# State space layer: dt x B partly from VectorE through PSUM, the product with C wholly on GpSimd, and a new table of half groups

**Chip, cores, metric.** One core of one Trainium2 chip. The metric is the device time of one execution in microseconds (us), median of several runs on the same chip.

## The reference, cut to what matters

Two layers run one after the other. The first is a selective state space layer on 4 images of 64 x 64 positions (4 x 4096 steps in time, 768 inner channels, 16 states), the second a windowed attention. The change touches only the first:

```python
dt = softplus(einsum('blr,dr->bld', dt, dt_w) + dt_b)
def step(h, inp):                     # over the 4096 positions
    dA  = exp(dt_t[:, :, None] * A[None])
    dBx = (dt_t * x_t)[:, :, None] * B_t[:, None, :]
    h   = dA * h + dBx
    y_t = einsum('bdn,bn->bd', h, C_t)
y = y + xc * D;  y = y * silu(z);  out = einsum('bld,cd->blc', y, out_proj_w)
```

## The kernel before

The code here is cut and condensed. In the profiles the engines are DVE (VectorE), POOL (GpSimd), ACT (ScalarE), PE (TensorE) and SP (SyncE); da is the decay exp(dt A), db the product dt x B, hp and hs the state h, and L96 a helper through which most activations go. A hole is time in which the DVE stands idle before a scan.

A step of the kernel is one of 64 chunks of 256 positions (T). In a step there are 24 groups: 6 blocks of 128 channels (d) by 4 groups (g) of 4 states. A group is two half groups of two states; a slot of the schedule is one half group, so a step has 48 slots. All else (projections, convolution, Silu, softplus, output projection of other steps) is hung on these slots, and each engine works its list in order: in the stretch from 2,000 to 4,000 us of the changed kernel's trace the 159 instructions of ACT in a step come in the same order in 19 of 21 steps (the other two have two of a group norm more), GpSimd's 64 in 20 of 21 (the other has a memset in place of a copy).

```python
ps_a bufs=2; ps_h bufs=1; ps_y bufs=2; ps (work banks) bufs=3      # PSUM, 8 buffers

def driven(I, d, g, h):               # dt x B: GpSimd, all 24 groups, [128, 4*256]
    nc.gpsimd.tensor_tensor(db, h["dtx"].unsqueeze(1).broadcast_to([P, NG, T]), h["bc"][g][0], ALU.mult)

def scan(I, d, g, h, db, y, ahead):
    for half, to in ((0, hp), (1, hs)):           # hp in PSUM, hs in SBUF
        da = ps_a.tile([P, 2, T], F32, tag="da")
        for k in range(2):
            act(da[:, k, :], dt, AF.Exp, scale=nega[:, d, n + k : n + k + 1])      # decay
        for k in range(2):
            nc.vector.tensor_tensor_scan(to[:, k, :], da[:, k, :], db[:, 2 * half + k, :], ...)
            if half == 1 and k == 0:
                nc.vector.tensor_copy(state[:, d, n - 2 : n], hp[:, :, T - 1])
                nc.vector.tensor_tensor(hv, hp, ct[:, 0:2, :], ALU.mult)           # C, first half
        ahead()                                   # the other work of this slot
    def with_c():                                 # C, second half: GpSimd
        nc.gpsimd.tensor_copy(state[:, d, n : n + 2], hs[:, :, T - 1])
        nc.gpsimd.tensor_tensor(hs, hs, ct[:, 2:4, :], ALU.mult)
# TensorE sums hv and hs over the states by transposing products into one PSUM tile y per d
# ... slots: x 0-9, conv 11-20, z 20-27, Silu burst 29, softplus 33 + 3q, out_proj 8-10 ...
```

Of the kernel before, what the change touches and what calls it, by code (L numbers as in the profile page):

```python
# [14 lines left out]
P = 128  # L15
C = 384
# [32 lines left out]
def two_layers(  # L49
# [221 lines left out]
    def layer0(x1s, mvs, gms1):  # L271

        with ExitStack() as es:
            es.enter_context(tc.manual_schedule(engines=in_step))
            ps_a = es.enter_context(tc.tile_pool(name="ps_a", bufs=2, space=PSUM))
            ps_h = es.enter_context(tc.tile_pool(name="ps_h", bufs=1, space=PSUM))
            ps_y = es.enter_context(tc.tile_pool(name="ps_y", bufs=2, space=PSUM))
            ps = es.enter_context(tc.tile_pool(name="ps0", bufs=3, space=PSUM))
# [3 lines left out]
            gms, gbs, st1s = {}, {}, {}  # L282

# [17 lines left out]
            def next_batch(b, at):  # L301
# [15 lines left out]
                for n in range(NJ * NXT):  # L317
                    t, j = divmod(n, NJ)
                    at(24 * n + 17, lambda t=t, j=j: load(t, j))
                    at(24 * n + 29, lambda t=t, j=j: nc.vector.bn_stats(st[:, j, t, :], h["x"]))  # L320
# [8 lines left out]
            def normed(I, h, at):  # L329
# [3 lines left out]
                def load():  # L333
                    h["x"] = w2.tile([P, NJ, T], F32, tag="xi", name=f"xi_{b}_{i}", bufs=3)
                    nc.sync.dma_start(
                        h["x"],
                        x[b, :, i * T : (i + 1) * T].rearrange("(k p) t -> p k t", p=P),
                    )
# [30 lines left out]
                at(20, load)  # L369
                at(30, by_group)  # L370
                at(31, lambda: mean("xn", "mu"))
                at(32, lambda: with_row("mu", ALU.subtract))
                at(34, square)
                at(35, lambda: mean("sq", "var"))
                at(37, root)
                at(38, lambda: with_row("var", ALU.mult))
# [21 lines left out]
            def prepared(I, h, at):  # L398
# [13 lines left out]
                def pair(key, first, tile):  # L412
                    def one(k):
                        if k == 0:
                            h["pb"][key] = bank()
                        tile(h["pb"][key], k)

                    at(first, lambda: one(0))
                    at(first + 1, lambda: one(1))

                at(0, kept)
                for p in range(ND // 2):
                    d = 2 * p
                    pair(("x", p), 3 * p, lambda pb, k, d=d: in_proj(pb, k, d + k, h["xn"]))
                    at(3 * p + 3, lambda p=p, d=d: with_bias(
# [8 lines left out]
                    pair(("c", p), 11 + 3 * p, lambda pb, k, d=d: conv(pb, k, d + k))  # L434
                    at(14 + 3 * p, conv_out)

                    def z_out(p=p, d=d):
                        z = w2.tile([P, 2, T], F32, tag="sz", name=f"sz_{b}_{i}_{d}", bufs=5)
                        with_bias(z, h["pb"][("z", p)], binp[:, ND + d : ND + d + 2])
                        h["sz"].append(z)  # L440

                    pair(
                        ("z", p), 20 + 2 * p,
                        lambda pb, k, d=d: in_proj(pb, k, ND + d + k, h["xn"]),
                    )
                    at(23 + 2 * p, z_out)
# [6 lines left out]
                def x_proj():  # L453
                    h["pd"] = bank()
                    for d in range(ND):
# [5 lines left out]
                def rows():  # L461
# [5 lines left out]
                    h["bc"] = []  # L467
                    for g in range(NS // NG):
                        both = []
                        for tag, r0 in (("B", 0), ("C", NS)):  # L470
                            t = bc.tile([P, NG, T], F32, tag=tag, name=f"{tag}_{b}_{i}_{g}")
                            src = rows[r0 + g * NG : r0 + (g + 1) * NG, :]
                            nc.sync.dma_start(t, src.unsqueeze(0).broadcast_to([P, NG, T]))
                            both.append(t)
                        h["bc"].append(both)

                at(29, burst)
                at(30, x_proj)
                at(32, rows)

                def softplus(q, first):
# [27 lines left out]

                    def added():  # L510
                        pb, dt = t["pb"], t["dt"]
                        nc.vector.scalar_tensor_tensor(
                            pb, pb, -1.0, t["e"], ALU.add, ALU.subtract
                        )
                        nc.vector.tensor_tensor(pb, t["r"], pb, ALU.subtract)
                        nc.vector.tensor_tensor(dt, dt, pb, ALU.add)
                        h["dt"].append(dt)

                    at(first, project)
                    at(first + 2, parts)  # L520
                    at(first + 3, exped)
                    at(first + 4, logged)
                    at(first + 5, added)

                for q in range(ND // 2):
                    softplus(q, 33 + 3 * q)

            def driven(I, d, g, h):

                b, i = divmod(I, NCHUNK)  # L530
                if g == 0:
                    h["dtx"] = w2.tile([P, T], F32, tag="dtx", name=f"dtx_{b}_{i}_{d}")
                    nc.gpsimd.tensor_tensor(
                        h["dtx"], h["dt"][d // 2][:, d % 2, :], h["xc"][d // 2][:, d % 2, :],
                        ALU.mult,
                    )
                db = w2.tile([P, NG, T], F32, tag="db", name=f"db_{b}_{i}_{d}_{g}", bufs=3)
                nc.gpsimd.tensor_tensor(  # L538
                    db, h["dtx"].unsqueeze(1).broadcast_to([P, NG, T]), h["bc"][g][0], ALU.mult
                )  # L540
                return db

            def scan(I, d, g, h, db, y, ahead):



                dt = h["dt"][d // 2][:, d % 2, :]
                ct = h["bc"][g][1]
                hp = ps_h.tile([P, 2, T], F32, tag="hp", name="hp")
                hv = w2.tile([P, 2, T], F32, tag="hv", name="hv")  # L550
                hs = w2.tile([P, 2, T], F32, tag="hs", name="hs", bufs=4)
                for half, to in ((0, hp), (1, hs)):
                    da = ps_a.tile([P, 2, T], F32, tag="da", name="da")
                    n = g * NG + 2 * half
                    for k in range(2):
                        act(da[:, k, :], dt, AF.Exp, scale=nega[:, d, n + k : n + k + 1])
                    for k in range(2):
                        nc.vector.tensor_tensor_scan(  # L558
                            to[:, k, :], da[:, k, :], db[:, 2 * half + k, :],
                            state[:, d, n + k : n + k + 1] if I % NCHUNK else 0.0,  # L560
                            ALU.mult, ALU.add,
                        )
                        if half == 1 and k == 0:
                            nc.vector.tensor_copy(state[:, d, n - 2 : n], hp[:, :, T - 1])
                            nc.vector.tensor_tensor(hv, hp, ct[:, 0:2, :], ALU.mult)  # L565
                    ahead()

                def with_c():
                    nc.gpsimd.tensor_copy(state[:, d, n : n + 2], hs[:, :, T - 1])  # L569
                    nc.gpsimd.tensor_tensor(hs, hs, ct[:, 2:4, :], ALU.mult)  # L570

                def summed(t):

                    for k in range(2):
                        first = g == 0 and t is hv and k == 0
                        last = g == NS // NG - 1 and t is hs and k == 1
                        for half in range(2):
                            nc.tensor.matmul(  # L578
                                y[:, half, :], t[:, k, half * P : (half + 1) * P], ident,
                                is_transpose=True, start=(first and half == 0),  # L580
                                stop=(last and half == 1), skip_group_check=True,
                            )

                return with_c, lambda: summed(hv), lambda: summed(hs)

            def turned(I, d, h, yt):

                ys = w2.tile([P, 2, P], F32, tag="ys", name=f"ys_{I}_{d}")
                nc.scalar.copy(ys, yt)
                y = bank()[:, 0, :]  # L590
                for half in range(2):
                    nc.tensor.matmul(
                        y[:, half * P : (half + 1) * P], ys[:, half, :], ident,
                        is_transpose=True, start=(half == 0), stop=False,
                        skip_group_check=True,
                    )
                nc.tensor.matmul(
                    y, dsd[:, d, :], h["xc"][d // 2][:, d % 2, :], start=False, stop=True,
                    skip_group_check=True,
                )  # L600
# [534 lines left out]
```

## Time and profile before

| | before |
|---|---|
| time | 9,142 us (9,140 to 9,145) |
| scans run | 112 us to 6,800 us of the span |
| one step | 104.8 us: DVE busy 93.8, POOL 93.8, PE 83, ACT 71.1 |
| DVE idle in a step | 11.0 us |

The lines are in the prediction below: of the products of 128x512, GpSimd's took 1,269 ns and hv on the DVE, with one operand in PSUM, 681, a ratio of 1.86. All 458 hv of the stretch from 2,000 to 4,000 us took 669 to 685 ns, with GpSimd busy 90% of it. One view it does not show is what ACT waited for in the same stretch (19.1 steps); columns: us in total, times, longest.

```profile
ACT da L96 <- DVE hs L558: 288.8, 270, 3.0
ACT da L96 <- DVE hp L558: 100.1, 201, 2.0
ACT xc L96 <- PE mm_ps L388: 94.4, 19, 5.4
ACT spe L96 <- PE mm_ps L488: 76.7, 19, 4.8
ACT xb L96 <- PE mm_ps L381: 33.5, 36, 1.7
```

The first two lines are harmless: ACT is early and waits for a decay buffer. The next three are not: once a step ACT stands 5 us for the convolution, 4 us for softplus and under 2 us for the projection, the decay behind them in its list is late, and the DVE waits. Measured slot by slot in the trace (idle of the DVE just before the scans of a slot, mean of 55 steps), the holes of before are 3.0 us at slot 15 (convolution), 3.7 at 30 and 31 (Silu burst), 2.5 at 37 to 39 (softplus) and 0.7 at 4.

### The profile page before, as it was taken

How to read it: one execution, taken by the hardware profiler on the slowest of the kernel's cores; microseconds unless marked ns; L12 is line 12 of the kernel's file. 1: busy time of each engine (PE TensorE's matmuls, PEld its weight loads, DVE VectorE, ACT ScalarE, POOL GpSimd, SP SyncE). 2: the span in 40 equal slices, each digit the busy share in tenths (PEclk: the TensorE clock that was granted, in tenths of full speed). 3: DMA queues.
4: the chain of work that ended last, by engine and by line, in shares of the span. 5: the costliest groups of instructions: out<-in, count | busy, mean ns of one | idle time of the engine just before them, and what ended most of it. 6: DMA issues, size and time to landing. Idle time of an engine off the chain costs nothing. (4 is left out here: it accounts for less than half of the span.)

```text
span 9134.5 us, 141565 instructions
## 1 busy us (share of the span) xinstructions
PE 7574.6 (83%) x45882; PEld 5681.8 (62%) x45882; DVE 7496.7 (82%) x15604; ACT 5711.1 (63%) x13566; POOL 7650.8 (84%) x6679
## 2 busy tenths in 40 slices
PE   6877778877778877778877788777879999999999
PEld 5666666666666666666666666666655555555555
DVE  6898888898889888988988888888876666666666
ACT  4666666666666666666666666666644545455454
POOL 5998888988889898889888989988976767777677
PEclk8888878888888888788888788888879999999999
DMA  3111111111111111111111111111112222232222
GB/s 100 53 49 51 54 61 48 48 49 51 58 59 50 50 45 52 59 55 53 49 48 49 58 45 48 45 45 56 51 65 84 89 82 87 83 92 87 82 86 65
DMA packets 301929, 558.05 MB, mean 61 GB/s; under 512 B 61916, under 2 KB 185580, under 8 KB 301060
## 3 DMA queue, kind: packets, MB, share of 16 engines
q1 hardware_dynamic: 301188, 549.00, 18.7%
q8 instruction: 364, 5.96, 0.3%
q14 instruction: 377, 3.09, 0.1%
HBM read 446.33 MB, written 84.73 MB: 58 GB/s over the span
## 5 line engine op out<-in xcount | busy, mean ns | idle before, releaser
L96 ACT ACTIVATE da<-dt,nega 128x256 f32<-128x256 f32 x6144 | 2922.7, 477 | 1425.6 <-DVE hs L558 976.4
L538 POOL TENSOR_TENSOR db<-dtx,B 128x1024 f32<-128x1024 f32 x1536 | 3618.1, 2356 | 30.1
L558 DVE TENSOR_TENSOR_SCAN hp<-da,state,db 128x256 f32<-128x256 f32 x2880 | 2155.8, 749 | 304.5 <-POOL state L569 193.3
L558 DVE TENSOR_TENSOR_SCAN hs<-da,state,db 128x256 f32<-128x256 f32 x2880 | 2121.5, 737 | 341.2 <-ACT da L96 341.1
L911 POOL TENSOR_SCALAR sg<-sg,rsum 128x308 f32<-128x308 f32 x1536 | 1619.8, 1073 | 633.2 <-DVE rsum L909 631.2
L570 POOL TENSOR_TENSOR hs<-hs,C 128x512 f32<-128x512 f32 x1536 | 1949.1, 1269 | 123.2 <-POOL state L569 0.8
L578 PE MATMUL y<-ident,hv 128*128 128x128 f32 x6144 | 1192.7, 328 | 962.0 <-DVE hv L565 956.0
L578 PEld LDWEIGHTS y<-ident,hv 128*128 128x128 f32 x6144 | 850.9, 165 | 1403.5 <-DVE hv L565 1288.1
L578 PE MATMUL y<-ident,hs 128*128 128x128 f32 x6144 | 1156.4, 321 | 139.4 <-POOL hs L570 137.9
L381 PE MATMUL mm_ps<-xn,w_in 128*128 128x256 f32 x4608 | 1166.7, 405 | 2.0 <-DVE xn L357 2.0
L565 DVE TENSOR_TENSOR hv<-hp,C 128x512 f32<-128x512 f32 x1536 | 1046.2, 681 | 0.0
L578 PEld LDWEIGHTS y<-ident,hs 128*128 128x128 f32 x6144 | 902.5, 169 | 185.4 <-POOL hs L570 182.9
L381 PEld LDWEIGHTS mm_ps<-xn,w_in 128*128 128x128 f32 x4608 | 928.8, 208 | 133.0 <-issue 2.7
L96 ACT ACTIVATE sg<-sg,mx 128x308 f32<-128x308 f32 x1536 | 828.7, 541 | 250.5 <-DVE mx L896 234.3
L896 DVE CUSTOM_DVE_ANT_0 sg<-lg_ps,bias 128x308 f32<-128x308 f32 x1536 | 643.1, 475 | 375.0 <-PE lg_ps L890 375.0
L569 POOL COPY state<-hs 128x2 f32<-128x2 f32 x1536 | 287.0, 187 | 533.3 <-DVE hs L558 472.7
L388 PE MATMUL mm_ps<-xb,dcv 128*128 128x256 f32 x3072 | 717.5, 380 | 0.0
L388 PEld LDWEIGHTS mm_ps<-xb,dcv 128*128 128x128 f32 x3072 | 568.8, 190 | 71.4
L939 ACT COPY tb<-pt_ps 88x512 f32<-88x512 f32 x384 | 221.8, 578 | 625.3 <-PE pt_ps L935 625.2
L488 PE MATMUL mm_ps<-xd,w_dt 24*128 24x256 f32 x768 | 331.2, 572 | 291.8 <-DVE yg L605 288.9
L616 PE MATMUL mm_ps<-yg,w_out 128*128 128x256 f32 x2304 | 519.0, 380 | 0.0
L926 DVE COPY ta<-pt_ps 110x512 f32<-110x512 f32 x768 | 492.5, 682 | 23.3 <-PE pt_ps L921 23.3
(145 smaller groups left out, 10490.4 us busy)
## 6 DMA issues: line engine op xcount, KB each, us to landing
B<-bcrows SPq DMA_DIRECT2D x256, 512.0 KB
C<-bcrows SPq DMA_DIRECT2D x256, 512.0 KB
vw<-vd SPq DMA_DIRECT2D x1792, 33.0 KB
xr<-x SPq DMA_DIRECT2D x28, 1056.0 KB
vd<-v SPq DMA_DIRECT2D x280, 96.0 KB
xi<-in_x_dram SPq DMA_DIRECT2D x64, 384.0 KB
x<-xo SPq DMA_DIRECT2D x64, 384.0 KB
o<-x SPq DMA_DIRECT2D x96, 256.0 KB
```

Of the source, the lines that this page charges most:

```text
L96: ins = nc.scalar.activation(o, i, func, **kw)
L381: nc.tensor.matmul(pb[:, k, :], w_in[:, j, m * P : (m + 1) * P], xn[:, j, :], start=(j == 0), stop=(j == NJ - 1),)
L388: nc.tensor.matmul(pb[:, k, :], dcv[:, d, c, :], xb[:, d, c : c + T], start=(c == 0), stop=(c == KC - 1),)
L538: nc.gpsimd.tensor_tensor(db, h["dtx"].unsqueeze(1).broadcast_to([P, NG, T]), h["bc"][g][0], ALU.mult)
L558: nc.vector.tensor_tensor_scan(to[:, k, :], da[:, k, :], db[:, 2 * half + k, :], state[:, d, n + k : n + k + 1] if I % NCHUNK else 0.0, AL ...
L565: nc.vector.tensor_tensor(hv, hp, ct[:, 0:2, :], ALU.mult)
L570: nc.gpsimd.tensor_tensor(hs, hs, ct[:, 2:4, :], ALU.mult)
L578: nc.tensor.matmul(y[:, half, :], t[:, k, half * P : (half + 1) * P], ident, is_transpose=True, start=(first and half == 0), stop=(last an ...
L616: nc.tensor.matmul(h["po", first][:, m - first, :], w_out[:, d, m * P : (m + 1) * P], h["yg"][d], start=(d == 0), stop=(d == ND - 1),)
L896: nc.vector.tensor_tensor_reduce(sg[:, hh, :], lg[:, :NK], bias[:, 4 * m + hh, :], -1.0, BIG, ALU.add, ALU.min, mx[:, hh : hh + 1],)
L911: nc.gpsimd.tensor_scalar(sg[:, hh, :], sg[:, hh, :], rs[:, hh : hh + 1], None, ALU.mult)
L926: nc.vector.tensor_copy(t[: KN[0], :, :].rearrange("p a q -> p (a q)"), pt[: KN[0], :])
```

## The change

Intent: even out DVE and POOL, and fill the DVE's holes. VectorE makes dt x B for 15 groups, from a copy of dt x in PSUM; all four scans of a group go to SBUF and GpSimd multiplies them by C in one instruction; y is summed for two channel blocks at a time, so that its two PSUM buffers become one and the work banks go from three to four; and every slot in the table is new. The core of the diff, condensed (a "..." or a list of slots stands for several lines). Left out are more buffers (db from 3 to 6, hs from 4 to 5), which no run undoes, and the order in which B and C are loaded:

```diff
+            dtx_ps = ps_x.tile([P, 2, T], F32, name="dtx_ps")        # work banks: 3 -> 4
-                at(30, by_group) ... at(29, burst) ... at(33 + 3q: +2 parts, +3 exped, +4 logged, +5 added)
+                at(22, by_group) ... at(26, burst) ... at(34, 36, 46: +3 parts, +4 exped, +5 logged, +6, +7)
-                at(8 to 10, all 36 products of out_proj); at(12), at(13) residual
+                at(17, 18, 19, 20, 22, 23: six products each); at(26), at(28) residual
+            def dt_x_copied(d, h):
+                nc.scalar.copy(dtx_ps[:, d % 2, :], h["dtx"][d])
+            def driven(I, m, h, eng):
+                dtx = dtx_ps[:, d % 2, :] if eng is nc.vector else h["dtx"][d]
+                eng.tensor_tensor(db, dtx.unsqueeze(1).broadcast_to([P, NG, T]), h["B"][g], ALU.mult)
+            def with_c(I, m, h, hs):
+                nc.gpsimd.tensor_copy(state[:, d, g * NG : (g + 1) * NG], hs[:, :, T - 1])
+                nc.gpsimd.tensor_tensor(hs, hs, h["C"][g], ALU.mult)
+            driven_at = (          # (slot, 1 = VectorE, 0 = GpSimd) of groups 0 to 23
+                (-4, 0), (-1, 1), (1, 1), (2, 1), (4, 0), (7, 1), (8, 0), (10, 1),
+                (12, 0), (15, 1), (17, 1), (18, 1), (20, 0), (22, 1), (24, 0), (26, 1),
+                (26, 1), (26, 1), (30, 0), (33, 1), (36, 0), (39, 1), (40, 0), (43, 1),
+            )
+            dt_x_at = (-5, 2, 10, 18, 22, 34)
+                for half in range(2):          # the decay of the NEXT half group first,
+                    decay(*nxt, steps[nxt[0]]) # then scans, then the slot's other work
+                    scans(I, m, half, hs)
+                    run(I, 2 * m + half, 2 * m + half + 1)
```

## The prediction

> **What bounds the kernel now.** I read the page first. Its row of the DVE in 40 slices shows two stages: about 0.9 busy for some 30 slices (the state space layer), then 0.6 (attention).
>
> ```profile
> DVE  6898888898889888988988888888876666666666
> PE 22%; DVE 2%; issue 0%; POOL 0%; SPq 0%; DMA 0%; ACT 0%; POOLq 0%; DVEq 0%; ACTq 0%
> ```
>
> The second line, the chain that ended last, follows only the attention layer back (PE, 22% of the span), so it says nothing of the changed stage. The change touches only the first stage. In the trace the scans run from 112 us to 6,800 us, 64 steps of 24 groups; so I took the stretch from 2,000 to 4,000 us, all steady state. Its line in the view of windows (columns: PE, weight load, DVE, ACT, POOL, clock, DMA):
>
> ```profile
> 2000.00:4000.00 2000.00, 1590.08 (x7832) 1296.65 (x7831) 1789.00 (x3213) 1356.06 (x2977) 1790.01 (x1508) 0.82 0.16 53
> ```
>
> Next the groups by shape in the same stretch:
>
> ```profile
> L538 POOL TENSOR_TENSOR db<-dtx,B 128x1024 f32<-128x1024 f32 x458 | 1079.0, 2356 | 8.9
> L558 DVE TENSOR_TENSOR_SCAN hp<-da,state,db 128x256 f32<-128x256 f32 x867 | 648.9, 748 | 89.8 <-POOL state L569 56.5 <-ACT da L96 8.9 <-POOL db L538 3.4
> L558 DVE TENSOR_TENSOR_SCAN hs<-da,state,db 128x256 f32<-128x256 f32 x867 | 638.6, 737 | 105.0 <-ACT da L96 105.0
> L570 POOL TENSOR_TENSOR hs<-hs,C 128x512 f32<-128x512 f32 x458 | 581.2, 1269 | 36.7 <-POOL state L569 0.2
> L565 DVE TENSOR_TENSOR hv<-hp,C 128x512 f32<-128x512 f32 x458 | 311.9, 681 | 0.0
> L569 POOL COPY state<-hs 128x2 f32<-128x2 f32 x458 | 85.7, 187 | 164.3 <-DVE hs L558 145.2 <-PE y L578 19.1
> ```
>
> 458 groups at 24 a step are 19.1 steps, so one step is 104.8 us. Per step the DVE is busy 1789/19.1 = 93.8 us and idle 11.0; POOL is busy 93.8, ACT 71.1, PE 83. DVE and POOL are level, but nearly all that the DVE waits for before a scan is the decay exp(dt A) of ACT, not POOL's product: by the idle column 4.7 us a step before hp and 5.5 before hs. The part put down to the POOL copy of the state is ACT too, as the timeline shows:
>
> ```profile
> 2999.71 1.14 ACT L96 ACTIVATE sz<-sz 128x512 f32<-128x512 f32 x2
> ...
> 3000.86 1.28 ACT L100 ACT_TABLE_LOAD   x1
> 3002.16 0.99 ACT L96 ACTIVATE da<-dt,nega 128x256 f32<-128x256 f32 x2
> ...
> 3002.86 0.19 POOL L569 COPY state<-hs 128x2 f32<-128x2 f32 x1
> ...
> 3003.23 1.55 DVE L558 TENSOR_TENSOR_SCAN hp<-da,state,db 128x256 f32<-128x256 f32 x2 [3.01 <-POOL state L569]
> ```
>
> Once a step ACT runs its burst (six Silu of 0.62 us, two table loads of 1.28 us: 6.3 us); the decay comes only after it, ends at 3003.15, and the scan starts at 3003.23. That is 3 us of DVE idle a step. So the stage is bound by the DVE at 90%, with holes that ACT makes.
>
> How much of the DVE's time one instruction really takes is read from start to start, as the ends overlap:
>
> ```profile
> 3199.94 1.52 DVE L558 TENSOR_TENSOR_SCAN hp<-da,state,db 128x256 f32<-128x256 f32 x2
> 3201.37 0.72 DVE L558 TENSOR_TENSOR_SCAN hs<-da,state,db 128x256 f32<-128x256 f32 x1
> 3202.01 0.13 DVE L564 COPY state<-hp 128x2 f32<-128x2 f32 x1
> 3202.07 0.68 DVE L565 TENSOR_TENSOR hv<-hp,C 128x512 f32<-128x512 f32 x1
> 3202.66 0.74 DVE L558 TENSOR_TENSOR_SCAN hs<-da,state,db 128x256 f32<-128x256 f32 x1
> 3203.32 1.53 DVE L558 TENSOR_TENSOR_SCAN hp<-da,state,db 128x256 f32<-128x256 f32 x2
> ```
>
> A pair hp costs 1.43, an hs 0.65, the copy 0.06, hv 0.59: 3.38 us a group. 24 groups are 81.1; the rest of a step (gate products 6 x 0.33, nine softplus parts of 0.60, two norm rows of 0.86, statistics 1.9, residual 0.9) is 11.9. Sum 93.0, against 93.8 measured: the sum is good to 1%.
>
> [...] The scans and hv here read one operand in PSUM[...]: hv takes 681 ns beside a busy POOL. This is why the change copies dt x into PSUM before the DVE multiplies it by B. [...]
>
> **The change, part by part, per step.**
> DVE loses 24 hv (24 x 0.59 = 14.2) and 24 copies of the state (1.4), and the pairs hp their extra 0.11 (a wait of the second on the DVE itself; 2.7). It gains 15 products of 128x1024: [...] Gate products become three of 512 columns (3 x 0.60 for 6 x 0.33: -0.2). 93.8 - 14.2 - 1.4 - 2.7 + 16.9 - 0.2 = 92.2 us. So the floor of the DVE falls by under 2 us.
> POOL: the rows for 256, 512 and 1024 columns (728, 1269, 2356 ns) lie on one line, 185 ns plus 2.12 ns a column. Before: 24 x 2.356 + 24 x 1.269 + 24 x 0.187 + 6 x 0.728 = 95.9. After: 9 products with B (21.2), 24 whole products with C (56.5), copies 4.5, dt x 4.4: 86.6. POOL loses 9 us and stops being level with the DVE.
> ACT gains six copies of dt x to PSUM (6 x 0.37 = 2.2), loses about 0.5 on the three larger copies of y: 73.
> PE does the same products and transposes. DMA reads x once more (384 KB a step) at a 16% share: nothing.
> The larger part is **the holes.** In the build of the changed kernel the DVE has, at the slot of the burst, three products with B, a norm row and a residual between one half group's scans and the next: 3.4 + 0.9 + 0.6, with two half groups of scans 2 x 1.31, some 7.5 us, against 1.0 + 6.3 + 1.0 of ACT from the release of the decay buffer. I expect 0.5 us left of 3. Elsewhere I summed ACT and DVE slot by slot over the 48 half groups: 0.96 of decay against 1.31 of scans, plus what each slot has. ACT gains on the DVE almost everywhere; it loses ground in slots 37 to 39 (three softplus parts of 1.87, 1.2 and 0.6 us with hardly any filler on the DVE: 3.4 us, of which the two decay buffers cover about 1), and by about 1.2 us in slots 11 to 14 and 19 to 20. That leaves about 3 us of stalls from ACT's own work, the burst included, and I add 1.5 for decay that comes late because ACT waits for PE or for dt x from POOL (before, ACT waited for PE 5 us a step for xc and 4 us for softplus). Idle 4.5.
> Sum: 92.2 + 4.5 = 96.7 us a step; (104.8 - 96.7) x 64 = 518 us. 9,142 - 518 = 8,624; I say **8,640 us**, as first and last steps gain less. Attention keeps its 2,330 us.
>
> **Rivals.**
> (a) The DVE's holes stay at 11 us: ACT is in order, still has two decay buffers, and waits for PE. For it: the same buffers and the same 46 us of decay. Against: respaced slots, a fourth work bank, fillers at the burst. Then 103.2 us a step and 9,040 us.
> (b) POOL becomes what is waited for: a group with both products costs it 2.36 + 0.19 + 2.36 = 4.9 us, and its product with B is due four half groups later, 5.24 us of scans. Thin, though five buffers of h and six of dt x B absorb one late group. PE's transposes now all wait for POOL, where half had waited for the DVE; a late PE holds up ACT. If so, 99 to 101 us and 8,770 to 8,900.
> (c) The DVE's products contend with POOL after all and take 2.2 us instead of 1.2: 15 more us, 112 a step, 9,600. The trace of hv speaks against it.
> (d) Nearly all holes close: 94 us, 8,450.
>
> **Range and chances.** 8,450 is (d), 8,870 the upper half of (b). To miss a gain of 2% (above 8,959) a step must stay above 101.9, so holes of nearly 10 us: (a), 0.07. Slower needs (c) or an unseen serial wait: 0.02. Faster 0.91.
>
> **What would show it.** Per step in the profile after: DVE product with B 1.2 us (2 or more means contention); scans to hs near 737 ns; POOL product with C 2.36 us, POOL's busy share down to 0.88 or so; DVE busy share up to about 0.95, with the waits for the decay halved or better and the hole at the burst under 1 us. If the DVE's waits before scans name POOL's product or PE, (b) holds; if they still name the decay with some 10 us a step, (a). The prediction is wrong if step times lie outside 94 to 100.5 us.

## The result

**8,366 us** (8,360 to 8,368, four runs) against 9,142 of before on the same chip: ratio 0.915, 95% interval 0.913 to 0.917. Ratios are the mean time of one kernel's fast runs over that of the other's of the same rounds, so not quite the ratio of the medians quoted. The direction was right; the kernel is faster than the whole range of the prediction (8,450 to 8,870).

The scans now end at 6,020 us instead of 6,800; these 780 us are the whole gain of 777 us in the spans (9,134.5 to 8,357.8). The window line of the changed kernel, same columns as in the prediction:

```profile
2000.00:4000.00 2000.00, 1686.96 (x8840) 1397.68 (x8838) 1965.77 (x2863) 1574.44 (x3440) 1840.09 (x1382) 0.89 0.19 64
```

The groups by shape of the changed kernel in the same stretch (count | busy us in total, mean ns of one | idle of the engine just before them, and what ended it):

```profile
L571 DVE TENSOR_TENSOR_SCAN hs<-da,state,db 128x256 f32<-128x256 f32 x1976 | 1322.5, 728 | 28.0 <-ACT da L96 20.2 <-POOL hs L581 5.2
L581 POOL TENSOR_TENSOR hs<-hs,C 128x1024 f32<-128x1024 f32 x518 | 1221.6, 2358 | 41.7
L550 POOL TENSOR_TENSOR db<-dtx,B 128x1024 f32<-128x1024 f32 x195 | 460.7, 2363 | 0.0
L550 DVE TENSOR_TENSOR db<-dtx_ps,B 128x1024 f32<-128x1024 f32 x323 | 384.0, 1200 | 0.0
```

518 groups are 21.6 steps, so a step takes 92.7 us (104.8 before; 92.5 from scan to scan, as in the table below). Per step: DVE busy 91.1 and idle 1.6; POOL 85.3; ACT 73.0; PE 78. PE's granted clock in the stretch rose from 0.82 to 0.89, which may have helped its results to come in time; no run separates this from the spacing. Idle before scans fell from 195 us in the stretch (prediction, 89.8 + 105.0) to 28. What the DVE still waits for, and then what ACT waits for; its waits for PE have all but gone:

```profile
DVE hs L571 <- ACT da L96: 23.5, 29, 1.2
DVE hs L571 <- POOL hs L581: 5.2, 21, 0.3
ACT da L96 <- DVE hs L571: 368.8, 528, 2.1
ACT dtx_ps L543 <- POOL dtx L537: 16.4, 23, 1.8
ACT xb L96 <- PE mm_ps L382: 1.3, 1, 1.3
```

and at the burst the DVE has work, as this stretch of the time line of the changed kernel shows (start, length, engine; lines of ACT and the DVE, without the Silus):

```profile
3028.45 0.99 ACT L96 ACTIVATE da<-dt,nega 128x256 f32<-128x256 f32 x2 [0.21 <-DVE hs L571]
3029.46 1.28 ACT L96 ACT_TABLE_LOAD   x1
3029.62 0.66 DVE L653 TENSOR_TENSOR xo<-mm_ps,xo 128x512 f32<-128x512 f32 x1
3030.20 3.47 DVE L550 TENSOR_TENSOR db<-dtx_ps,B 128x1024 f32<-128x1024 f32 x3
...
3033.60 0.94 DVE L358 TENSOR_TENSOR xn<-xn,mm_ps 128x768 f32<-128x768 f32 x1
3034.00 1.28 ACT L100 ACT_TABLE_LOAD   x1
3034.46 1.38 DVE L571 TENSOR_TENSOR_SCAN hs<-da,state,db 128x256 f32<-128x256 f32 x2
3035.30 1.90 ACT L96 ACTIVATE da<-dt,nega 128x256 f32<-128x256 f32 x4
3036.39 0.75 DVE L571 TENSOR_TENSOR_SCAN hs<-da,state,db 128x256 f32<-128x256 f32 x1 [0.55 <-ACT da L96]
```

From the start of the first table load to the end of the second ACT makes no decay for 5.8 us; the DVE fills it with a residual, three products and a norm row and then waits 0.55 us, where before it waited 3.01.

What is left by slot in the changed kernel: 0.87 us at slot 39, 0.27 at 22, 0.24 at 28, 0.14 at 15.

### The profile page after: what moved, and what is told of

Its sections match the earlier page's. It is cut to its first block, busy times and chain, and to the rows that moved or that the text cites. A ratio compares the mean times of both kernels' runs of the same rounds, so it can differ in the third digit from the quotient of the medians.

```text
span 8357.8 us, 139186 instructions
## 1 busy us (share of the span) xinstructions
PE 7252.0 (87%) x45882; PEld 5495.0 (66%) x45882; DVE 7311.7 (87%) x13300; ACT 5812.2 (70%) x13758; POOL 7092.7 (85%) x5719
## 5 line engine op out<-in xcount | busy, mean ns | idle before, releaser
L571 DVE TENSOR_TENSOR_SCAN hs<-da,state,db 128x256 f32<-128x256 f32 x5760 | 3855.0, 728 | 88.9 <-ACT da L96 64.8
L581 POOL TENSOR_TENSOR hs<-hs,C 128x1024 f32<-128x1024 f32 x1536 | 3621.7, 2358 | 123.9 <-POOL state L580 0.4
L594 PE MATMUL y<-ident,hs 128*128 128x128 f32 x12288 | 1774.6, 296 | 904.5 <-POOL hs L581 902.3
L594 PEld LDWEIGHTS y<-ident,hs 128*128 128x128 f32 x12288 | 1540.5, 153 | 1207.9 <-POOL hs L581 1098.9
L550 POOL TENSOR_TENSOR db<-dtx,B 128x1024 f32<-128x1024 f32 x576 | 1360.5, 2362 | 0.1
L550 DVE TENSOR_TENSOR db<-dtx_ps,B 128x1024 f32<-128x1024 f32 x960 | 1141.3, 1199 | 0.0
L580 POOL COPY state<-hs 128x4 f32<-128x4 f32 x1536 | 289.1, 188 | 341.8 <-DVE hs L571 328.0
L639 PEld LDWEIGHTS mm_ps<-yg,w_out 128*128 128x128 f32 x2304 | 439.6, 195 | 59.1
L951 PE MATMUL pt_ps<-ident,sg 128*110 128x128 f32 x3072 | 417.7, 279 | 0.8 <-POOL sg L941 0.8
L951 PEld LDWEIGHTS pt_ps<-ident,sg 128*110 128x110 f32 x3072 | 322.7, 133 | 77.9 <-issue 47.6
```

Source lines behind the costliest of these rows:

```text
L550: eng.tensor_tensor(db, dtx.unsqueeze(1).broadcast_to([P, NG, T]), h["B"][g], ALU.mult)
L571: nc.vector.tensor_tensor_scan(hs[:, j, :], da[:, k, :], dbs[I, m][:, j, :], state[:, d, n : n + 1] if I % NCHUNK else 0.0, ALU.mult, ALU.add,
L581: nc.gpsimd.tensor_tensor(hs, hs, h["C"][g], ALU.mult)
L594: nc.tensor.matmul(y[:, d % 2, half, :], hs[:, k, half * P : (half + 1) * P], ident, is_transpose=True, start=(first and half == 0 and d % ...
L639: nc.tensor.matmul(h["po", first][:, m - first, :], w_out[:, d, m * P : (m + 1) * P], h["yg"][d // 2][:, d % 2, :], start=(d == 0), stop=( ...
L951: nc.tensor.transpose(pt[: KN[c], col : col + P], sg[:, 2 * pair + hh, KOFF[c] : KOFF[c] + KN[c]], ident,)
```

## The experiments

Fifteen kernels, all correct, all profiled in the fast state. Steps are from scan to scan in the traces, mean of 56 steps; each ratio is to the kernel of before on the same chip. The edits are shown condensed.

| run | edit | time, us | ratio to before | step, us |
|---|---|---|---|---|
| (changed kernel) | | 8,366 | 0.915 | 92.5 |
| e1_no_fill | the three products leave the burst | 8,583 | 0.939 | 96.0 |
| e2_old_table | new split, old slots | 9,132 | 0.999 | 104.8 |
| e3_old_split | old split, new slots | 8,751 | 0.958 | 98.6 |
| e4_14_groups | 14 on VectorE, group 10 moved | 8,497 | 0.930 | 94.5 |
| e5_14_other | 14 on VectorE, group 19 moved | 8,395 | 0.918 | 92.9 |
| e6_13_groups | 13 on VectorE | 8,435 | 0.923 | 93.5 |
| e7_short_gaps | PE's results read a slot earlier | 8,468 | 0.926 | 94.1 |
| e8_dtx_sbuf | no copy of dt x to PSUM | 9,106 | 0.996 | 104.0 |
| e9_fill_38 | a product from slot 39 to 38 | 8,352 | 0.914 | 92.3 |
| e10_fill_14 | e9 and 14 on VectorE | 8,362 | 0.915 | 92.4 |
| e11_three_banks | three work banks | 8,374 | 0.916 | 92.7 |
| e12_decay_last | decay after the slot's other work | 8,610 | 0.942 | 96.3 |
| e13_out_lumped | out_proj in a lump | 8,524 | 0.932 | 95.0 |
| e14_old_spread | e2 with out_proj spread | 9,072 | 0.992 | 103.8 |
| e15_softplus_38 | e9, second softplus later | 8,353 | 0.913 | 92.3 |

**Split or table?** My theory was that the gain lies in the holes and the table closes them; the rival, that the split gives GpSimd slack and that closes them. e2 keeps the split and undoes the slots:

```diff
-  at(22, by_group) ... at(35, ...)        +  at(30, by_group) ... at(38, ...)
-  at(26, burst), x/conv/z slots new       +  at(29, burst), x/conv/z slots of before
-  first in (34, 36, 46): +3 +4 +5 +6 +7   +  first in (33, 36, 39): +2 +3 +4 +5 +5
-  out_proj at 17 to 23, residual 26, 28   +  out_proj at 8 to 10, residual 12, 13
```

> The new split of the work, with the slots of before for everything that TensorE and ScalarE prepare (projections, convolution, norm, Silu burst, softplus, output projection, turning of y); the products dt x B stay in the new table's slots. Theory T (the table closed the holes, the split only moved work): the holes of before in slots 15, 30 and 37 to 39 return, 8 to 9 us a step, 92.6 becomes 100 to 101, about 8,870 us. Rival S (the split closed them, as GpSimd has slack now): 93 to 95 us a step, 8,400 to 8,520 us.

Measured: 9,132 us, ratio 0.999. Work fell (DVE busy about 92 us a step), but the holes are all back, at slots 16 (2.0 us), 22 (1.0), 31 and 32 (5.0) and 37, 38 (2.2), and a new wait of the DVE joins them, the residual for PE. From the lists of waits of e2, of the DVE and then of ACT:

```profile
DVE hs L570 <- ACT da L96: 176.1, 103, 4.4
DVE xo L652 <- PE mm_ps L638: 41.4, 33, 1.6
ACT xc L96 <- PE mm_ps L389: 90.4, 20, 4.8
```

So the split in the old slots is worth nothing: what it saves, the waits take. (One reserve: the three products for the burst stayed in slot 26 while the burst went back to 29, so they could not fill it. But even without that hole of 5 us, 64 x 5 = 320 us by my estimate, e2 would be far from the 8,400 to 8,520 of the rival.) The rival is refuted. The softplus hole also stays, 2.2 us, although ACT's wait for PE before it is gone (3.2 us in the stretch, 76.7 before): there it is mostly ACT's own work. e3 is the opposite:

```diff
+  nc.vector.tensor_tensor_scan(hs[:, j, :] if half else hp[:, k, :], ...)
+  nc.vector.tensor_tensor(hs[:, 0:2, :], hp, C[:, 0:2, :])     # first half
-  nc.gpsimd.tensor_tensor(hs, hs, C)
+  nc.gpsimd.tensor_tensor(hs[:, 2:, :], hs[:, 2:, :], C[:, 2:, :])
+  driven_at = ((2 * m - 4, 0) for m in range(24));  no dtx_ps
```

> The new table with the old split: GpSimd makes dt x B for all 24 groups, VectorE multiplies the first half of h by C from PSUM, GpSimd the second half; no copies of dt x to PSUM. Theory T: holes mostly closed though there is no product left to fill the burst, VectorE 93 us of work a step plus 3 at the burst plus 1.5, 97 to 98 us, about 8,700 us, unless GpSimd (94 to 96 us of work) is itself waited for. Rival S: as before the change, 104 us a step, about 9,100 us.

Measured: 8,751 us, a step of 98.6, close to theory T. The table with the old split: 6 us a step; e2 and e3 both keep the rest of the change (buffers, banks, decay ahead), so what the buffers do for the table is not shown. Split on top of the new table: another 6, of which 2.1 is work (e3: DVE busy 93.2) and 3.9 holes: e3 still waits 2.8 us at the burst, for want of products to fill it, and about 1.5 us a step (31.3 us in the stretch) for GpSimd's dt x B. So the split pays only where the table gives its pieces a place.

**The burst.** e1 moves the fillers and nothing else:

```diff
-  (26, 1), (26, 1), (26, 1)      # groups 15, 16, 17
+  (28, 1), (30, 1), (32, 1)
```

> The changed kernel, but the three products dt x B that VectorE makes in slot 26, beside ScalarE's burst of Silu and table loads, are moved to slots 28, 30 and 32, where they are just in time. Same work on every engine. Theory F (these products fill VectorE's hole at the burst, 3.2 us a step before): the hole before the scans of slot 28 comes back with about 3 us a step, time 8,366 + 64 x 3 = 8,560 us. Rival (the hole closed because VectorE is now the fuller engine and ScalarE runs ahead; the place of the products does not matter): within 40 us of 8,366.

Measured: 8,583 us; the hole at slot 28 goes from 0.24 to 3.43 us and the step grows by 3.4. In the list of waits of e1 the decay takes 86.7 us where the changed kernel has 23.5:

```profile
DVE hs L571 <- ACT da L96: 86.7, 44, 3.9
```

**PE's results in time.** Three parts of the table concern this: the gap between PE's product and ACT's reading, the fourth bank, and the lump of the output projection. e7 shortens all gaps by one slot:

```diff
-  at(x[2], ...); at(c[2], ...); at(z[2], ...); softplus +3 +4 +5 +6 +7
+  at(x[2] - 1, ...); at(c[2] - 1, ...); at(z[2] - 1, ...); softplus +2 +3 +4 +5 +6
```

> The changed kernel, with ScalarE's reading of every pair of TensorE's results (projection, convolution, gate, softplus) one slot earlier, so that two slots lie between the second product and its reading, as before the change, not three. Theory G (the longer gaps are what ended ScalarE's waits for TensorE, about 10 us a step before the change): waits of xb, xc and spe for TensorE return, 2 to 4 us of holes a step, 8,490 to 8,620 us. Rival (the order of the table as a whole did it, or the fourth bank, and the gap is not needed): within 40 us of 8,366.

8,468 us: 1.6 us a step, holes 3.1 instead of 1.6. That is below the lower end of what I gave, and not by the path of theory G. ACT's waits for PE rise only to 25 us in the stretch, none of them for xc or softplus; the largest of e7:

```profile
ACT sz L96 <- PE mm_ps L382: 17.5, 21, 1.9
```

Slot by slot, the new holes (0.5 us at slot 14, 0.6 more at 38 and 39, 0.4 at 47) are not behind these waits, which come at slot 18 (z) and at 41 and 42 (x). In each of 56 steps a reading (z, softplus, x) now stands together with a copy of dt x just ahead of the decays of slots 14, 38 and 47 in ACT's list. So e7 shows that these slots matter, but by the trace because of ACT's own work that falls together; that the longer gap to PE is needed is not shown. e11:

```diff
-  ps = tile_pool(name="ps0", bufs=4, space=PSUM)
+  ps = tile_pool(name="ps0", bufs=3, space=PSUM)
```

> The changed kernel with three PSUM banks for TensorE's results, as before the change, not four. Theory: a product then waits for the bank's last reader, ScalarE gets its results late; 1 to 4 us a step, 8,430 to 8,620 us. Rival (three are enough with the new slots): within 30 us of 8,366.

8,374 us: no difference that these runs can tell. The fourth bank, for which y was summed in pairs, is not needed with the new slots. e13 and e14 take the output projection:

```diff
 e13, in the changed kernel                       e14, in e2
-  out_proj at 17, 18, 19, 20, 22, 23             -  out_proj at 8, 8, 9, 9, 10, 10
+  out_proj at 10, 10, 11, 11, 12, 12             +  out_proj at 17, 18, 19, 20, 22, 23
-  residual at 26, 28                             -  residual at 12, 13
+  residual at 14, 15                             +  residual at 26, 28
```

> The changed kernel with the output projection's 36 products in slots 10 to 12 in a lump, beside the convolution's and the gate's, instead of spread over slots 17 to 23; residual in 14 and 15. Theory L (before, the lump made TensorE late for the convolution and so ScalarE for the decay: the hole of 3 us at slot 15): ScalarE waits for xc or sz again and a hole of 2 to 3 us a step comes, 8,490 to 8,570 us. Rival (the lump does no harm, as the gaps are longer now): within 40 us of 8,366.

> The kernel with the old slots and the new split (9,132 us), but with the output projection alone spread over slots 17 to 23 as in the new table. Theory L: the waits of ScalarE for xc (4.7 us a step) and of VectorE for the residual (2.2) go, the hole at slot 16 closes, about 4 us a step, 8,880 us. Rival: other parts of the old table keep ScalarE waiting in the same places, above 9,050 us.

e13: 8,524 us, 2.5 us a step: the size expected, but by luck, as it comes by another path. The hole grew little (0.6 us more at slot 28); most of it is the DVE itself waiting for the residual (line 1, of e13's DVE), while ACT's wait for z (line 2, e13's ACT) is absorbed. The residual was moved with the lump, close behind it, so the lump by itself costs less than 2.5 us:

```profile
DVE xo L653 <- PE mm_ps L639: 40.3, 42, 2.0
ACT sz L96 <- PE mm_ps L382: 64.9, 23, 3.2
```

e14: 9,072 us; theory L gave 8,880 and fails. The wait for xc fell from 90 to 26 us and the residual's is gone, but the projections of z sit in slots 20 to 27 of the old table, and there ACT now waits (ACT's waits in e14):

```profile
ACT sz L96 <- PE mm_ps L382: 140.5, 59, 4.0
ACT xc L96 <- PE mm_ps L389: 25.7, 21, 1.8
```

The hole at slot 16 closed and the one at 22 grew from 1.0 to 2.3 us. It stands behind what is left of the wait for xc (1.2 us a step, at slot 21) and the copies of y and dt x just ahead of it; the waits for z cost little (0.7 us at slots 27 and 29). So the lump alone did not make the holes of e2.

**The order on ACT.** e12 issues the next decay after the slot's other work, as before the change:

```diff
-  decay(next); scans(now); run(slot)
+  scans(now); run(slot); decay(next)
```

> The changed kernel with the decay of the next half group issued after the other work of the slot on ScalarE, as before the change, not ahead of it. The order of decay and other work is the same but for a shift by one half group, so ScalarE's own sums stay; it reads TensorE's results one decay earlier, 1 us. Expected as with the shorter gaps: 8,366 to 8,470. If the order itself closed the holes: 8,600 or more.

8,610 us, 3.8 us a step: my expectation (at most 8,470) was wrong. I had argued that the order is the same but for a shift. By the trace most of the cost is that shift of one half group: ACT reaches each copy of dt x one half group earlier, before GpSimd has made it. Its wait there (ACT's waits in e12) is 4.8 us a step, 0.8 in the changed kernel:

```profile
ACT dtx_ps L543 <- POOL dtx L537: 99.6, 59, 2.7
```

Behind these waits stand holes of 1.1 us at slots 13 and 14 and of 1.5 at 25 and 27. Another 1.4 us came at slots 37 to 40, beside softplus. No further run separates the two.

**dt x in SBUF.** e8 lets VectorE read dt x from SBUF:

```diff
-  dtx = dtx_ps[:, d % 2, :] if eng is nc.vector else h["dtx"][d]
+  dtx = h["dtx"][d]              # and no copy to PSUM
```

> The changed kernel without the copy of dt x into PSUM: VectorE's product reads both operands from SBUF[...]. ScalarE loses six copies, 2.2 us a step. Theory P[...]: the VectorE product takes 2 us or more instead of 1.2, or GpSimd's products lengthen, 10 to 20 us a step, 9,000 to 9,600 us. Rival (no contention for this shape): 1.2 us, 8,320 to 8,370 us.

9,106 us. With GpSimd busy 96% of the stretch, the groups of e8 beside those of the changed kernel above: the DVE product takes 1,913 ns instead of 1,200, GpSimd's product with B 2,569 instead of 2,363, with C 2,424 instead of 2,358.

```profile
L576 POOL TENSOR_TENSOR hs<-hs,C 128x1024 f32<-128x1024 f32 x462 | 1119.7, 2424 | 37.2
L545 DVE TENSOR_TENSOR db<-dtx,B 128x1024 f32<-128x1024 f32 x290 | 551.8, 1913 | 0.0
L545 POOL TENSOR_TENSOR db<-dtx,B 128x1024 f32<-128x1024 f32 x174 | 446.9, 2569 | 0.0
```

15 x 0.71 us = 10.7 of the 11.5 us that a step grows. A rival is that a product with both operands in SBUF is slower by itself. The trace of e8 speaks against it: of its 289 DVE products in the stretch 91 took 1.19 to 1.25 us, as in the changed kernel (1.19 to 1.22 in all 323), the others up to 3.39, and single products of GpSimd took up to 3.44 where 2.39 was the most. So with both operands in SBUF each time a product took 1.2 us in some places and up to 3.39 in others, and some of GpSimd's grew too: the operands by themselves are not what costs. By what path the two engines lengthen each other's products is not shown. Without the six copies to PSUM, 0.37 us each on ACT, nearly the whole gain is lost.

**Is 15 the right number?** With the DVE busy 98%, one product less should gain 1.1 us a step.

```diff
 e4:  (17, 1) -> (16, 0)                                     # group 10
 e5:  (33, 1) -> (28, 0), dt x of block 5: 34 -> 32          # group 19
 e6:  e5 and (2, 1) -> (2, 0)                                # group 3
 e9:  (39, 1) -> (38, 1)                                     # group 21
 e10: e9 and (2, 1) -> (2, 0), dt x of block 2: 10 -> 6
 e15: e9, second softplus first = 36 -> 38
```

> The changed kernel with 14 of 24 products on VectorE: group 10 goes to GpSimd in slot 16. VectorE loses 1.13 us a step and GpSimd gains 2.36. If VectorE alone bounds the stage (98% busy), 91.5 us a step, 8,366 - 70 = 8,295 us. If GpSimd or the waits between the two bound it already at 85 us of work, 8,366 or more.

> Again 14 of 24 products on VectorE, but group 19 moves, to GpSimd's slot 28, where GpSimd is idle for 1.9 us a step, and the dt x of channel block 5 is made in slot 32 instead of 34, its copy stays in slot 36. Theory D (the run with group 10 moved lost because GpSimd, busy in slots 12 to 24, gave dt x late, ScalarE stood at its copy and the decay came late): no such wait here, VectorE has 1.13 us a step less to do, 8,366 - 60 = 8,305 us. Rival (GpSimd has no room for a tenth product anywhere): 8,420 or more.

> 13 of 24: group 19 as in the run before and group 3 on GpSimd in slot 2, where GpSimd is idle for 2.3 us a step in slots 2 and 4. GpSimd has 90 us of work, VectorE 88.9. If VectorE's work still sets the step: 8,366 - 120 = 8,245 us. If GpSimd's lateness shows (waits of scans for its products or for the freed buffers): 8,330 to 8,450.

> The changed kernel with one product of VectorE one slot earlier: group 21 in slot 38, not 39, ahead of the hole of 0.87 us that is left before the scans of slot 39, where ScalarE works off two softplus parts. Theory A (what is left of the holes is ScalarE's own work in that place, and a filler ahead of it closes it as at the burst): hole gone, 64 x 0.87 = 55 us, 8,310 us. Rival (the hole only moves to slot 40 or 41): within 15 us of 8,366.

> As the run before, and 14 products on VectorE: group 3 goes to GpSimd's slot 2, where GpSimd is idle for 2.3 us a step in slots 2 and 4, and the dt x of block 2 is made in slot 6, not 10, so that its copy in slot 12 does not wait. If GpSimd's lateness is the only price of a tenth product: 8,310 - 64 x 1.1 = 8,240 us. If, as in the two earlier runs with 14, something in GpSimd's queue comes late all the same: 8,310 to 8,400.

> The run with the product in slot 38, and the second softplus two slots later (38 instead of 36), so that ScalarE does not have the two right behind each other in slots 37 to 39. Theory A (the last hole is ScalarE's own work there): the 0.6 us hole at slot 40 shrinks by 0.4 or more, 8,352 - 30 = 8,320 us. Rival (it moves to slots 42 to 44, where the projections are read): 8,345 or more.

e4: 8,497 us, slower. Not for want of GpSimd's time (in the changed kernel it works 85 us a step and waits 5), but of place: the tenth product stands ahead of the dt x of blocks 3 and 4 in GpSimd's list, ACT waits for them (ACT's waits in e4), and holes of 3.4 us open in slots 20 to 26.

```profile
ACT dtx_ps L543 <- POOL dtx L537: 78.9, 43, 2.9
```

e5 puts the tenth product where GpSimd is idle: 8,395, a third of a per cent above the changed kernel, not 60 us below. Theory D was right on e4's wait, which is gone, but GpSimd now carries its lateness on to slot 36, and ACT waits 1.7 us a step for y, whose transposes wait for GpSimd (37.0 us in the stretch, none in the changed kernel). In e6 and e10, too, the further products on GpSimd come back as waits (holes of 4.4 us in e6; in e10 2.4 against 1.4 in e9). e9 and e15 end at 8,352 and 8,353 us, ratios 0.914 and 0.913 with intervals that overlap that of 0.915: no gain that these runs can tell. In both, the hole at slot 39 is gone and one of 0.6 us stands at slot 40. The view calls it "issue", but in both traces the scan there starts 0.09 us after the end of its decay, in each of 56 steps. On ACT this decay stands behind the first softplus (slots 37 and 38); e15 moved only the second, whose work comes after it. So e15 could not close this hole, and theory A is not tested by it. The table of the change is, within 15 us, as good as any that I tried.

## Why the prediction was wrong

Right were: which stage, that the DVE is and stays the bound, that its floor hardly falls and the gain is in the holes; product on the DVE 1.2 us (1.200); GpSimd's product with C 2.36 (2.358) and its fall to about 85 busy us (86.6 given; its share is 0.92 and not 0.88, as the step shrank more); ACT 73; a DVE product that stays as short with dt x in PSUM (1.200 us, GpSimd busy 92% of the stretch), and a longer one without it (e8: 1.913, GpSimd busy 96%); the burst hole nearly closed by three products (e1). None of the rivals happened; it went beyond (d), the rival in which nearly all holes close.

The step that failed is "**Idle 4.5**" in "Sum: 92.2 + 4.5 = 96.7 us a step". Measured: 91.1 + 1.6 = 92.7. The difference, 4.0 us in 64 steps, is 256 us of the 274 by which 8,640 was too high; 2.9 of the 4.0 are idle time that did not come. Its parts:

- **The wait for PE and for dt x, 1.5 us: no hole is left of it.** ACT waits 1.3 us for PE in the whole stretch, and for dt x 0.8 us a step, at slots 24 and 25, behind which the DVE has no hole. (The 0.27 us at slot 22 end with GpSimd's product with C, 5.2 us in the stretch, a wait that the sum did not have.) I had named the respaced slots against rival (a) only and gave them no credit in the sum. Where an experiment brings such waits back, they cost: in e12 about 2.5 us of holes stand behind copies of dt x, in e13 the DVE waits 1.9 us for the residual. What the longer gaps alone are worth is not shown (e7).
- **ACT's own work, 3 us: measured about 1.3** (0.87 at slot 39, 0.24 at the burst, 0.14 at 15). I counted the DVE from start to start but ACT by the length of its instructions. This is to be seen in the trace of before, in the stretch that I had read (time line of ACT):

```profile
3012.82 0.45 ACT L96 ACTIVATE spe<-mm_ps,dtb 128x256 f32<-128x256 f32 x1
3013.18 0.46 ACT L96 ACTIVATE spr<-mm_ps,dtb 128x256 f32<-128x256 f32 x1
3013.54 0.47 ACT L96 ACTIVATE spe<-mm_ps,dtb 128x256 f32<-128x256 f32 x1
3013.89 0.48 ACT L96 ACTIVATE spr<-mm_ps,dtb 128x256 f32<-128x256 f32 x1
3014.25 1.00 ACT L96 ACTIVATE da<-dt,nega 128x256 f32<-128x256 f32 x2
```

  They are 0.47 long but 0.36 apart: four take 1.43 us, not the 1.87 of the prediction. That is an overlap of 110 ns; the two decays of a tile have none (the last line: 1.00 us for two of 0.48). The slots 37 to 39, which I summed to a loss of 3.4 us, give 2.4 that way (1.09 + 0.84 + 0.45, an estimate from the spacings of the changed trace), less the 1 us of the two buffers 1.4: nearer to the 0.87 measured. This makes up 1.0 of the 1.7 us; the rest stays open. By length the instructions of ACT in a step of the changed kernel add to 79 us, where I wrote 73 from the busy time; a check of the one against the other would have shown it. Two terms also do not follow from the numbers beside them: at the burst 8.3 - 7.5 leaves 0.8 us and not 0.5 (measured 0.24), and 1.87 + 1.2 + 0.6 is 3.67 and not 3.4.
- **Work of the DVE, 92.2: measured 91.1.** I carried along the 0.8 us by which my sum by parts fell short of the busy time before; with start-to-start times of the changed trace (96 scans x 0.647, 15 products x 1.119 and the rest 12.2) the sum is 91.1. The 16.9 us for the 15 products was my estimate (measured 16.8). It can be worked out from the trace of before: DVE products of 512 columns took 681 ns and of 768 columns 944, 1.03 ns a column, so hv's 0.59 us and 512 columns more give 1.12 us, an estimate, and 15 of them 16.8.

What stays open: how the table's parts add up. e1, e7, e12 and e13 undo 3.4 + 1.6 + 3.8 + 2.5 = 11.3 us one at a time, more than the 9.4 us by which idle fell, so they overlap, and e14 shows that a part put in alone can do little (60 us).

## What to carry to other kernels

When two engines are level and each is 10% idle, moving work between them can be worth little until the waits have a place to be filled: here the split in the old slots gave 0.1%, the new table with the old split 4%, both 8.5%. Count every engine of a schedule by start-to-start spacing, not by instruction length (ACT here: 79 us a step by length, 73 busy), and check that the sum agrees with the busy time of the page. Look at the place of a small operand that others wait for, here dt x on GpSimd: in e4, with a long product ahead of it, ACT waited 78.9 us for it in the stretch and the step grew by 2.0 us, although GpSimd had had 5 us a step to spare.
